# Random-feature attention with a mixture of experts on one core: copies of normalized rows issued by GpSimd, and two counts in one PSUM bank

## The chip, the cores and the metric

The kernel runs on one core of one Trainium2 chip. A core has TensorE (PE, matrix products into PSUM), VectorE (DVE), ScalarE (ACT), GpSimd (POOL) and SyncE (SP, which here only issues DMAs), all with queues of their own. ScalarE and GpSimd can issue DMAs too. The metric is the device time of one execution in microseconds, lower is better.

## The reference

The input is 8192 tokens of 512 numbers. Cut to what matters:

```python
xn = layernorm(x)
feats = rfs(xn)                       # 512 features: exp of a projection less a norm
attn  = feats @ weights.T             # weights: the same features of 512 input rows
# the mixture of experts
scores = sigmoid(xn @ router_w)       # 64 experts in 8 groups
#   the best 4 groups, in them the best 8 experts per token; their weights sum to 2.5
#   each expert takes its first 256 tokens, in order of tokens
dispatch[e, pos] = xn[token]
expert_out = (silu(dispatch @ gate_w) * (dispatch @ up_w)) @ down_w
moe = sum of weight * expert_out, and a shared expert on all tokens
out = x + attn + moe
```

The position of a token in an expert is a running count over all earlier tokens. Everything is float32.

## The kernel before

**Precision.** A matmul operand is split into a high part (rounded to float32r by a ScalarE copy, `upper`, line 98) and a residual (VectorE, `rest`, line 101). `products` (line 108) adds three products: high by high, high by low, low by high.

**Stages.** Tokens go in 16 blocks of 512. In the first stage, up to some 405 us, the routing of every block is computed (`look_up`, lines 343 to 484) and, for the even blocks, the shared expert and the attention (`dense`, lines 513 to 565). The second stage, up to some 1161 us, runs the 64 experts: GpSimd gathers an expert's rows by indirect DMA (`gather`), TensorE transposes and multiplies them, and GpSimd adds the results to the output by indirect DMA. The attention of odd blocks (`late_attention`) is spread over it. The third finishes the odd blocks.

**The order of work.** `look_up` and `dense` are generators that one loop advances by hand: `routing` (line 841) is called once per step of `dense`, advances every open `look_up` by one step, begins a new one every five steps, and two steps before that calls `normalize` for it. So a pair of blocks, an odd one and the next even one, passes during the ten steps of one even block's `dense`. What is written this way sets priorities. The tile library then fixes the order of instructions on each engine when the program is built, gives out the buffers of a pool in the order of the program, and sets the semaphores. On the chip each engine keeps to its order, and a DMA that waits holds up what is behind it on the engine that issues it.

**A block's path.** `statistics` (VectorE) and `roots` (line 281: 17 small operations on GpSimd) give a token's scale and shift. ScalarE writes the normalized rows into `xw` (line 301); a row has 577 numbers, since the router's results and a sum come behind the 512. From block 5 on (`ROUND`), each of a block's two `xw` tiles (two times 128 rows) is copied within SBUF into a tile `xc` of 512 columns by a DMA that ScalarE issues (line 314). The copy is of type float32 and is read as float32r by the transposes (line 331, tile `ps_x`), 16 a block. From there on the block is `xT`, high and low parts, two of whose four PSUM buffers come from the pool `ps_sm`.

One step later the router's matmul fills `ps_l` (line 364), copied to `lt` by ScalarE (line 374), transposed back into `ps_lt` (line 381), and VectorE finds groups and experts (lines 397 to 438): `mask_r` says who takes which expert, `prior_r` counts takers in the partition's rows before. Two steps later TensorE makes two sums of these: `ps_b` (line 443), each expert's count before each group of 128 tokens, and `ps_u` (line 454), the count up to each token, transposed. ScalarE copies `ps_u` to `cu` (line 462) and SP stores it. In the next step VectorE adds comparisons of `ps_b` to `begun` (line 482, two operations), from which the second stage finds each expert's tokens.

**PSUM.** The pools have 2, 4 and 2 banks. `ps_sm`, with two, holds in turn two `ps_x`, `ps_b`, `ps_u`, the next block's `ps_l` and its `ps_lt`: six tiles a block, all with the tag "sm".

Of the kernel before, what the change touches and what calls it, by code (L numbers as in the profile page):

```python
# [9 lines left out]
FP = mybir.dt.float32  # L10
# [8 lines left out]
P = 128  # L19
T = 8192  # L20
H = 512
R = 512
E = 64
# [8 lines left out]
TB = 512  # L32
NB = T // TB
NS = TB // P
# [19 lines left out]
def rfs_attention_moe_kernel(  # L54
# [15 lines left out]
    nc = tc.nc  # L70
# [6 lines left out]
    ps_sm = ctx.enter_context(tc.tile_pool(name="ps_sm", bufs=2, space=PSUM))  # L77
# [6 lines left out]
    def kib4(shape, name, dt=FPR):  # L84
        return four.tile(shape, dt, tag="four", name=name)
# [31 lines left out]
    def behind(a, b):  # L117

        tc.add_manual_dep(a.ins, b.ins.name, ORDER, reason="what a needs comes late")
# [38 lines left out]
    def store_rows(b, k, xb):  # L158

        r0 = b * TB + k * UT  # L160
        return nc.sync.dma_start(
            out[r0 : r0 + UT, :].rearrange("(s p) d -> p s d", p=P), xb.t[k]
        )
# [133 lines left out]
    def normalize(b, rstd, shift):  # L297
        xb = xbs[b]
        xw = [rows.tile([P, NH, XW], FP, tag="xw", name="xw") for _ in range(NS // NH)]
        for s in range(NS):  # L300
            normed_s = nc.scalar.activation(
                xw[s // NH][:, s % NH, :H],
                xb[s],
                AF.Identity,
                bias=shift[:, s : s + 1],
                scale=rstd[:, s : s + 1],
            )
            behind(normed_s, last["upper"])
        xc = None
        if b >= ROUND:  # L310

            xc = [kib4([P, NH, H], "xc", FP) for _ in xw]
            for t, w in zip(xc, xw):
                nc.scalar.dma_start(t, w[:, :, :H])
        if b % 2:

            for k in range(TB // UT):
                store_rows(b, k, xb)
            del xbs[b]
        return xw, xc  # L320
# [22 lines left out]
    def look_up(b):  # L343
# [90 lines left out]
        for s in range(1, NS):  # L434
# [4 lines left out]
        yield  # L439
        yield  # L440

        pb = ps_sm.tile([P, NS, E], FP, tag="sm", name="ps_b")
        counted = nc.tensor.matmul(
            pb.rearrange("p s e -> p (s e)"),
            ones_r,
            prior_r.rearrange("p s e -> p (s e)"),
            start=True,
            stop=True,
        )
        behind(counted, last["pe"])  # L450
        pu = ps_sm.tile([P, NS // 2, P], FP, tag="sm", name="ps_u")
        for q in range(NS // 2):
            for part, (w, v) in enumerate(((mask_r, tri_r), (prior_r, ones_r))):
                nc.tensor.matmul(
# [172 lines left out]
    rest(rwp[:, :, 1, :], rw_sb, rwp[:, :, 0, :], nc.gpsimd)  # L627
    normed = {}
    normed[0] = normalize(0, *roots(0, statistics(xbs[0], NS * [last["rest"]]), nc.vector))
    first = last["shift"]  # L630
    roots1 = roots(1, statistics(xbs[1], NS * [first]))
# [20 lines left out]
    for rc in range(RC):  # L652
        pool, tag = ((ps_sm, "sm"), (ps_tr, "tr"))[rc // 2]
        ps_w.append(pool.tile([P, H], FP, tag=tag, name="ps_f"))
        projected(parts(wT, KC), rc, ps_w[rc])
    late = look_up(0)
    next(late)
    upper0 = last["upper"]
    sup = split(sgu[1], "gu", (upper0, last["rest"]))
    fw = Chunks(RC, "fw", FP)  # L660
    for rc in range(RC):
        exponents = exponent(fw[rc], wn, rc, ps_w[rc])
        behind(exponents, last["rest"])
    normed[1] = normalize(1, *roots1)
    eab = const.tile([P, RC], FP, name="eab")
    behind(nc.scalar.activation(eab, ab, AF.Exp), upper0)
# [174 lines left out]
    def routing(t):  # L841

        for b in sorted(fronts):
            if next(fronts[b], fronts) is fronts:
                del fronts[b]
        b, k = divmod(t + GAP, GAP)
        if k == (b == 1) and b < NB:
            fronts[b] = look_up(b)
            next(fronts[b])
        if k == GAP - 3 and b + 1 < NB:  # L850
            normed[b + 1] = normalize(b + 1, *roots(b + 1, statistics(xbs[b + 1])))
        if k == 1 and b + 2 < NB:
            xbs[b + 2] = load_tokens(b + 2)
# [141 lines left out]
```

## Time and profile before

| | us |
|---|---|
| median of 3 runs | 1320.38 |
| lowest and highest | 1320.17, 1323.96 |
| the profiled execution | 1324.84 |
| its span | 1323.1 |
| first stage, 33 to 405 us: PE busy | 363.93 of 372 |
| second stage, 405 to 1161 us: PE busy | 752.71 of 756 |
| third stage, 1161 to 1323 us: PE busy | 156.65 of 162 |
| first stage: DVE, ACT, POOL busy | 286.66, 165.07, 52.91 |

In the rows of a profile, a tile stands without its number. "out<-in xN" names what an instruction writes and reads and how many are taken together; a timeline row begins with its start and its length in us, and ends in brackets with the idle time before it and what ended that. "ACTq" and "SPq" are DMAs as issued by ScalarE and SP, "PEld" a weight load of TensorE. [...] A row of waits has the total in us, how many times, and the longest. TensorE's matmuls overlap, so that the length of a row is more than the time it takes from the next. TensorE's clock was granted at 0.998 of full speed.

### The profile page before, as it was taken

How to read it: one execution, taken by the hardware profiler on the slowest of the kernel's cores; microseconds unless marked ns; L12 is line 12 of the kernel's file. 1: busy time of each engine (PE TensorE's matmuls, PEld its weight loads, DVE VectorE, ACT ScalarE, POOL GpSimd, SP SyncE). 2: the span in 40 equal slices, each digit the busy share in tenths (PEclk: the TensorE clock that was granted, in tenths of full speed). 3: DMA queues.
4: the chain of work that ended last, by engine and by line, in shares of the span. 5: the costliest groups of instructions: out<-in, count | busy, mean ns of one | idle time of the engine just before them, and what ended most of it. 6: DMA issues, size and time to landing. Idle time of an engine off the chain costs nothing.

```text
span 1323.1 us, 21351 instructions
## 1 busy us (share of the span) xinstructions
PE 1300.0 (98%) x7648; PEld 1138.6 (86%) x7648; DVE 929.2 (70%) x1922; ACT 646.1 (49%) x1017; POOL 573.1 (43%) x670
## 2 busy tenths in 40 slices
PE   8999999999999999999999999999999999999998
PEld 6888787788788899999999999999999999988886
DVE  7978768768765677777677767777776776643555
ACT  5644443444332455656556556655565565540111
POOL 3122012012105667778667676767677754210000
PEclk9999999999999999999999999999999999999999
DMA  7665675675585989999999999999999999875995
GB/s 253 239 229 198 234 259 197 233 266 209 193 314 178 305 216 306 270 276 271 317 271 264 309 265 283 248 294 285 266 259 303 281 259 234 227 220 178 317 319 191
DMA packets 192313, 338.60 MB, mean 256 GB/s; under 512 B 15952, under 2 KB 87632, under 8 KB 192208
## 3 DMA queue, kind: packets, MB, share of 16 engines
q1 hardware_dynamic: 153456, 245.93, 54.1%
q0 software_dynamic: 32768, 79.78, 27.3%
q10 hardware_dynamic: 5984, 11.54, 2.5%
q8 instruction: 60, 0.98, 0.3%
q14 instruction: 45, 0.37, 0.1%
HBM read 220.66 MB, written 104.99 MB: 246 GB/s over the span
## 4 chain that ended last, share of the span: by engine, by line
PE 90%; DVE 4%; DMA 4%; ACT 1%; issue 1%; POOL 0%; SPq 0%; DVEq 0%; ACTq 0%
PE ps_gu L108 41%; PE ps_o L108 14%; PE ps_e L108 13%; PE ps_fu L108 6%; PE ps_y L108 5%; PE ps_f L108 3%; PE ps_t L769 3%; DMA xc<-xw 2%; PE ps_l L364 2%; PE ps_x L331 2%; DMA xb<-in_L_attn_x_dram 1%; DVE f L491 0%; DVE r L499 0%; DVE fT L101 0%; DVE st L275 0%
## 5 line engine op out<-in xcount | busy, mean ns | idle before, releaser
L819 POOL DMA_INDIRECT out_dram<-ye,who x128 | 225.5, 1762 | 186.5 <-ACT ye L818 136.4
L108 PE MATMUL ps_gu<-gT,gu_h 128*128 128x256 f32 x2048 | 291.3, 284 | 0.0
L108 PEld LDWEIGHTS ps_gu<-gT,gu_h 128*128 128x128 f32 x2048 | 268.6, 192 | 5.3 <-ACT gu_h L98 1.0
L699 POOL DMA_INDIRECT at<-upto,line x128 | 140.2, 1095 | 80.1 <-DMA q<-norms 41.4
L108 PE MATMUL ps_gu<-gT,gu_l 128*128 128x256 f32 x1024 | 167.3, 286 | 0.2 <-DVE gu_l L101 0.2
L101 DVE TENSOR_TENSOR gu_l<-gu,gu_h 128x1024 fp32r<-128x1024 f32 x128 | 155.6, 1218 | 6.9 <-ACT gu_h L98 6.9
L752 POOL DMA_INDIRECT xg<-xnw,who x128 | 143.1, 1118 | 39.0 <-issue 32.6
L108 PE MATMUL ps_e<-d_h,ehT 128*128 128x512 f32 x512 | 148.6, 392 | 0.0
L108 PEld LDWEIGHTS ps_gu<-gT,gu_l 128*128 128x128 f32 x1024 | 140.9, 192 | 0.7 <-DVE gu_l L101 0.4
L98 ACT CAST gu_h<-gu 128x1024 fp32r<-128x1024 f32 x128 | 132.5, 1058 | 0.0
L246 POOL TENSOR_TENSOR a<-rstd,ve 128x4 f32<-128x4 f32 x45 | 10.5, 233 | 272.0 <-DVE rstd L242 269.6
L98 ACT CAST ehT<-sg 128x512 fp32r<-128x512 f32 x64 | 39.8, 621 | 156.6 <-DVE sg L499 153.7
L818 ACT ACTIVATE ye<-ps_e,we 128x512 f32<-128x512 f32 x128 | 88.6, 695 | 56.4 <-PE ps_e L108 55.6
L108 PEld LDWEIGHTS ps_e<-d_h,ehT 128*128 128x128 f32 x512 | 94.7, 188 | 18.8
L499 DVE SCALAR_TENSOR_TENSOR sg<-sg,ps_gu 128x512 f32<-128x512 f32 x64 | 44.0, 688 | 68.4 <-PE ps_gu L108 68.2
L101 DVE TENSOR_TENSOR d_l<-d,d_h 128x1024 fp32r<-128x1024 f32 x64 | 78.3, 1224 | 7.6 <-ACT d_h L98 7.2
L101 DVE TENSOR_TENSOR gT<-ps_t,gT 128x512 fp32r<-128x512 f32 x128 | 83.2, 682 | 0.0
L101 DVE TENSOR_TENSOR ehT<-sg,ehT 128x512 fp32r<-128x512 f32 x64 | 44.4, 694 | 51.8 <-ACT ehT L98 51.8
L505 ACT ACTIVATE f<-f,ab 128x512 f32<-128x512 f32 x64 | 46.4, 725 | 69.3 <-DVE f L491 69.3
L108 PE MATMUL ps_o<-fW_h,fT 128*128 128x512 f32 x288 | 79.3, 392 | 0.2 <-ACT fT L98 0.2
L108 PE MATMUL ps_e<-d_l,ehT 128*128 128x512 f32 x256 | 79.4, 391 | 0.0
L108 PE MATMUL ps_o<-d_h,hT 128*128 128x512 f32 x256 | 78.3, 396 | 0.0
(180 smaller groups left out, 2513.6 us busy)
## 6 DMA issues: line engine op xcount, KB each, us to landing
gu<-in_L_ffn_gate_w_dram SPq DMA_DIRECT2D x64, 512.0 KB
gu<-in_L_ffn_up_w_dram SPq DMA_DIRECT2D x64, 512.0 KB
d<-in_L_ffn_down_w_dram SPq DMA_DIRECT2D x64, 512.0 KB
xnw<-xw SPq DMA_DIRECT2D x32, 577.0 KB
xb<-in_L_attn_x_dram SPq DMA_DIRECT2D x32, 512.0 KB
out_dram<-xb SPq DMA_DIRECT2D x32, 512.0 KB
xT_h<-turned SPq DMA_DIRECT2D x30, 512.0 KB
xT_l<-turned SPq DMA_DIRECT2D x30, 512.0 KB
```

The costliest lines, as they stand in the source:

```text
L98: return nc.scalar.copy(dst, src)
L101: return on.tensor_tensor(dst, src, hi.bitcast(FP), ALU.subtract)
L108: last["pe"] = nc.tensor.matmul(ps, w[c][a], v[c][b], start=(start and part == 0 and c == 0), stop=(stop and part == 2 and c == n - 1),)
L331: last["turn"] = nc.tensor.transpose(pr[:, ts(s, P)], src(s)[:, ts(kc, P)], ident if dt is FP else ident_r)
L364: logits = nc.tensor.matmul(pl, rwp[:, kc].rearrange("p t e -> p (t e)"), v[kc], start=(n == 0 and kc == 0), stop=(n == 1 and kc == KC - 1),)
L499: nc.vector.scalar_tensor_tensor(dst, dst, 0.5, u, ALU.mult, ALU.mult)
L505: nc.scalar.activation(f, f, AF.Exp, scale=ab[:, rc : rc + 1])
L699: nc.gpsimd.indirect_dma_start(out=at[:, e % TE, h, :], out_offset=None, in_=upto, in_offset=bass.IndirectOffsetOnAxis(ap=line[:, e, h : h ...
L752: nc.gpsimd.indirect_dma_start(out=xgs[e][:, h, :], out_offset=None, in_=xnw, in_offset=bass.IndirectOffsetOnAxis(ap=who[:, e, h : h + 1], ...
L769: turned_s = nc.tensor.transpose(pr[:, c, ts(h, P)], xr[:, h, ts(c2 * 2 + c, P)], ident_r)
L818: nc.scalar.activation(ye[:, h, :], po, AF.Copy, scale=wes[e][:, h : h + 1])
L819: now = nc.gpsimd.indirect_dma_start(out=out, out_offset=bass.IndirectOffsetOnAxis(ap=who[:, e, h : h + 1], axis=0), in_=ye[:, h, :], in_o ...
```

## The change

Two edits. In `normalize` the two copies of a block are issued from GpSimd's queue and no more from ScalarE's. In `look_up` one tile of one PSUM bank, 512 numbers wide, is taken from `ps_sm` in place of two tiles; its first half is `pb`, its second `pu`. The matmuls and their readers are the same.

```diff
             xc = [kib4([P, NH, H], "xc", FP) for _ in xw]
             for t, w in zip(xc, xw):
-                nc.scalar.dma_start(t, w[:, :, :H])
+                nc.gpsimd.dma_start(t, w[:, :, :H])
...
-        pb = ps_sm.tile([P, NS, E], FP, tag="sm", name="ps_b")
+        both = ps_sm.tile([P, 2, TB // 2], FP, tag="sm", name="ps_bu")
+        pb = both[:, 0].rearrange("p (s e) -> p s e", e=E)
         counted = nc.tensor.matmul(
-            pb.rearrange("p s e -> p (s e)"),
+            both[:, 0],
             ones_r,
             prior_r.rearrange("p s e -> p (s e)"),
             start=True,
             stop=True,
         )
         behind(counted, last["pe"])
-        pu = ps_sm.tile([P, NS // 2, P], FP, tag="sm", name="ps_u")
+        pu = both[:, 1].rearrange("p (q t) -> p q t", t=P)
```

## The prediction

> **What bounds the kernel now.** I read the page's busy shares first, then TensorE's waits, then the timelines around the two places that the change touches.
>
> ```profile
> PE 1300.0 (98%) x7648; PEld 1138.6 (86%) x7648; DVE 929.2 (70%) x1922; ACT 646.1 (49%) x1017; POOL 573.1 (43%) x670
> ...
> PE 90%; DVE 4%; DMA 4%; ACT 1%; issue 1%; POOL 0%; SPq 0%; DVEq 0%; ACTq 0%
> ```
>
> TensorE (PE) is the bound: busy 98% of 1323.1 us and 90% of the chain that ended last. So an edit is worth what it takes out of PE's idle time, some 23 us in all, and work taken off ScalarE (49%) is worth nothing by itself. All that the diff touches runs in the first third, where PE waits little; these are its waits from 33 to 405 us (PE's matmuls, and PEld, its weight loads):
>
> ```profile
> PEld ps_x L331 <- DMA xc<-xw: 5.7, 5, 1.6
> PEld ps_l L364 <- ACT cu L462: 4.5, 7, 0.6
> PEld ps_l L364 <- issue: 3.2, 5, 0.6
> ```
>
> Columns: total us, times, longest. The first row is the copy of normalized rows that lands after PE wants to transpose it. The next two stand ahead of the router's matmul (ps_l, L364), once a block. Both places are the diff's.
>
> **Part 1: the copies (L314).** There are 22, two in each of the blocks 5 to 15. They behave in two ways. In even blocks (6, 8, 10, 12, 14; here block 6):
>
> ```profile
> 134.81 1.54 ACT L301 ACTIVATE xw<-xb,shift,rstd 128x512 f32<-128x512 f32 x2
> ...
> 143.86 0.66 ACTq L314 DMA_DIRECT2D xc<-xw  x1
> ...
> 145.58 0.65 ACTq L314 DMA_DIRECT2D xc<-xw  x1
> ```
>
> The rows are ready at 136.35 (134.81 + 1.54), yet ScalarE issues the copies 7.5 and 9.2 us later, because they stand in its queue behind copies that wait for PE and VectorE (lt at 140.49, f at 143.10, L388 at 144.38). PE meets the second copy too early:
>
> ```profile
> 150.75 0.28 PE L331 MATMUL ps_x<-ident_r,xc 128*128 128x128 f32 x2
> 151.92 0.28 PE L331 MATMUL ps_x<-ident_r,xc 128*128 128x128 f32 x1 [0.89 <-DMA xc<-xw]
> ```
>
> By the matmuls' start records the five losses are 1.03, 1.64, 0.83, 0.92 and 1.32, sum 5.7 us, the PEld row's total. GpSimd has nothing to do then: its timeline ends at 125.27 with the roots of block 6 and goes on at 164.28. So it can issue at about 136.4. Block 6's transposes come at 150.75, 14 us later; no transfer in the numbers below takes so long. I take **-5.7 us** for the even blocks. What could still hold them there is the SBUF slot that a copy writes, if its last user is late; ScalarE's queue hides whether that is so now.
>
> In odd blocks (5 to 15; here block 7) it is the other way round:
>
> ```profile
> 172.04 0.60 ACTq L314 DMA_DIRECT2D xc<-xw  x1
> ...
> 178.39 1.47 PE L331 MATMUL ps_x<-ident_r,xc 128*128 128x128 f32 x16
> ```
>
> ScalarE issues as soon as the rows are there, PE needs them 6.35 us later and waits for nothing. But GpSimd is busy just then: it computes the roots of block 8 from 169.18 to 173.64 (17 operations of some 0.28 us). On that queue the second copy starts at 172.04 at the earliest and, if both go behind the roots, at 173.64 plus the first copy's issue, 175.6. What a plain copy from GpSimd costs, no row shows; the nearest are the gathers, which GpSimd issues too:
>
> ```profile
> 414.26 1.01 POOL L699 DMA_INDIRECT at<-upto,line  x1 [0.30 <-issue]
> ...
> 428.44 0.95 POOL L752 DMA_INDIRECT xg<-xnw,who  x1 [0.31 <-issue]
> ...
> 435.69 1.96 POOL L752 DMA_INDIRECT xg<-xnw,who  x1 [0.30 <-issue]
> ```
>
> Issuing takes 0.95 to 1.96 us. The first of these is the last of eight that VectorE waits for at 417.77: 3.5 us from issue to use, with the queues fairly empty. The second is used by PE at 435.06: 6.6 us, under load. An xc copy is 512 KB in 256 rows, more than either, so I allow 1 us more at the light end: 4.5 to 6.6 us. Landing is thus 176.5 at best (no loss) and 182.2 at worst (3.8 us lost). SP's stores start at 174.44, behind the copies if these are issued early. I take issue at 174.0 and 4.9 us, that is 178.9, **0.5 us lost in each of six odd blocks, +3.0 us**; the ends are 0 and about 23.
>
> [...] The rows: 0.95 us alone, 1.96 us at 435.69 while VectorE ran the residual of the weights (L101, two SBUF inputs) from 434.48 to 436.83, a factor of two. [...]
>
> Behind the copies on GpSimd stand the roots of the next block. Block 8's last shift is done at 173.17 and ScalarE uses it at 181.75: 8.6 us of slack against at most 3.9 us of issuing. Cost nothing; without that slack 3.9 us in five blocks. SP's queue keeps its own order, nothing is moved past it. ScalarE loses 22 issues of 0.60 us, 13.2 us, of an engine with idle time: nothing.
>
> **Part 2: one PSUM bank for ps_b and ps_u.** The pool has two banks. Now the two counts take both, and the next block's ps_l has to wait until one is read:
>
> ```profile
> 160.21 0.28 PE L454 MATMUL ps_u<-ones_r,prior_r 128*128 128x128 f32 x1
> 160.32 0.68 PE L108 MATMUL ps_o<-fW_l,fT 128*128 128x512 f32 x2
> 161.25 0.94 PE L364 MATMUL ps_l<-xT_h,rwp 128*128 128x512 f32 x3 [0.24 <-DVE xw L471]
> ```
>
> A 512-column matmul enters every 0.227 us (four from 158.68 to 159.59). Two from 160.32 would let the next in at 160.77; it enters at 161.25, just after begun (L482, done 161.10) or cu (L462, done 160.90) frees a bank. The idle figures count this twice over (PEld 0.6, PE 0.2); the start records give 0.38 to 0.41 us in 12 blocks and 0.25 in one, 5.0 us in all. With one bank for both counts, ps_l takes the other, whose last reader is the VectorE residual of the transposes, done at 158.0. So **-5.0 us**; the ends are 0 (if the low half of the transposes comes late instead) and 5.0.
>
> It adds a wait. [...] Now begun (160.13 to 161.10, VectorE) and cu (160.53 to 160.90, ScalarE) overlap, in different banks. [...] Behind it on VectorE stand statistics and the next f (L491), for which VectorE sat idle 3.49 us at 142.32; PE's accumulators wait for f. [...] The next taker of the shared bank is ps_lt, which needs the lt copy (163.37 to 163.96) anyway, later than begun. Cost nothing.
>
> **Sum.** The profiled execution took 1324.84 us, 1.7 around its span, and is 4.5 us (0.3%) over the median, 1320.38. 1324.84 - 5.7 - 5.0 + 3.0 = 1317.1; the same 7.7 us off the median give **1312.7 us**.
>
> **Rivals.** A change under 0.3% (4.0 us) can't be told from none, so faster is under 1316.4 and slower over 1324.3.
>
> (a) Both stalls go and odd copies cost 0 to 1 us each: 1309.7 to 1315.7, likeliest 1312.7. For it: the idle GpSimd in even blocks and the free bank. Against: one unmeasured latency. Chance 0.60.
>
> (b) The stall moves: odd copies cost 1.1 to 2.4 us each, 6.6 to 14.4, which eats the gain. For it: GpSimd's queue holds the next roots just then, and SP's 1.6 MB of stores at 174.44. Time about 1319. Chance 0.15.
>
> (c) The second part doesn't do what it says, as ps_l in PE's queue then waits for something else (xT_l, or VectorE held up by begun): 1320.4 - 5.7 + 3.0 = 1317.7. Against: xT_l is done 2 us before. Chance 0.10.
>
> (d) Slower: odd copies land late under load. It decides from 14.7 us in six blocks, 2.45 us each, that is a landing at 180.8 in block 7. With both issued behind the roots (175.6) and the loaded 6.6 us it is 182.2, 3.8 us in each: 1320.4 - 10.7 + 22.8 = 1332.5; a mean of this case is 1329. Against: PE's order is fixed when the program is built, and a transpose that is planned later lets other matmuls go ahead. Chance 0.15.
>
> **How the numbers follow.** Faster: nearly all of (a), a little of (b) and (c), 0.63. Same: most of (b) and (c), 0.21. Slower: (d) and the edge of (b), 0.16. The range, 1308.5 to 1324.3, leaves out (d) and a rest below, under 2 in 10; (a)'s own is 1309.7 to 1315.7.
>
> **What the new profile would show.** Right: no wait of ps_x for xc in even blocks, and copies issued within 1 us after the rows; no wait of ps_l for cu, and ps_l straight after ps_u; begun after cu. Wrong: a row of ps_x waiting for xc in odd blocks, five or six times over 1 us; copies on GpSimd taking over 2 us each; ScalarE's xw waiting longer for the shift; PE waiting for f.

## The result and the profile after

The changed kernel takes 1311.7 us (median of six runs, 1310.29 to 1317.16) against 1320.28 us for the kernel before in the same session (1319.47 to 1323.96): 0.9936 of the time, 95% interval 0.9919 to 0.9952. In a later session the ratio was 0.9923 (0.9902 to 0.9944). The forecast was 1312.7. The profiled execution took 1313.35 us, with a span of 1311.6.

The busy shares and the chain, then TensorE's waits from 33 to 405 us, of the kernel after (lines behind the first edit have moved by 2 or 3: `ps_b` and `ps_u` are now `ps_bu`, lines 445 and 456):

```profile
PE 1296.5 (99%) x7648; PEld 1138.3 (87%) x7648; DVE 925.1 (71%) x1922; ACT 645.5 (49%) x1017; POOL 582.4 (44%) x692
...
PE 89%; DVE 6%; DMA 2%; SPq 1%; issue 1%; ACT 1%; POOL 0%; ACTq 0%; DVEq 0%
```

```profile
PEld ps_bu L445 <- issue: 3.1, 6, 0.7
...
PE ps_bu L445 <- DVE prior_r L435: 1.0, 4, 0.3
PE ps_lt L381 <- ACT lt L374: 0.9, 2, 0.7
```

Both old rows are gone: no row shows `ps_x` waiting for a copy or `ps_l` for a bank. New ones have come: in six places TensorE reaches the counts (`ps_bu`) a little before VectorE has finished `prior_r`.

Block 6, an even one, on ScalarE, GpSimd and TensorE (three timelines of the kernel after):

```profile
133.18 1.55 ACT L301 ACTIVATE xw<-xb,shift,rstd 128x512 f32<-128x512 f32 x2
...
135.03 0.77 POOL L314 DMA_DIRECT2D xc<-xw  x1 [5.55 <-ACT xw L301]
136.93 0.72 POOL L314 DMA_DIRECT2D xc<-xw  x1 [1.12 <-ACT xw L301]
...
150.62 1.49 PE L331 MATMUL ps_x<-ident_r,xc 128*128 128x128 f32 x16
```

The first tile is ready at 134.73 and its copy is issued at 135.03. The sixteen transposes come in one piece, 14 us after the second copy's issue. Block 7, an odd one:

```profile
168.87 0.78 POOL L314 DMA_DIRECT2D xc<-xw  x1 [1.38 <-ACT xw L391]
169.67 0.21 POOL L246 TENSOR_TENSOR a<-rstd,ve 128x4 f32<-128x4 f32 x1
...
170.75 0.77 POOL L314 DMA_DIRECT2D xc<-xw  x1 [0.31 <-ACT top L467]
171.55 0.24 POOL L249 TENSOR_TENSOR rstd<-a,rstd 128x4 f32<-128x4 f32 x1
...
176.83 1.49 PE L331 MATMUL ps_x<-ident_r,xc 128*128 128x128 f32 x16
```

The copies stand before and among the roots of block 8, not behind them. GpSimd is idle for 1.38 us ahead of the first, until ScalarE's rows are there, and the root behind it goes only then. Both land 3.2 us after issue, the second at 173.95, and TensorE needs them at 176.83. Block 5 has no such room: its second copy, issued at 124.30, lands at 130.02, and the transpose that reads it starts at 130.06, 0.1 us late. Over all 22 copies, the view of the tile `xc` says:

```profile
L314 POOL DMA_DIRECT2D xc<-xw x22: 724/770/982, 122.9 to 358.7; - x22
...
DMA to landing us min/median/max: 3.2/4.6/7.2
```

The three numbers of the first row are the shortest, median and longest duration in ns: a plain copy holds GpSimd for 0.72 to 0.98 us. The counts and what follows, on TensorE, then on ScalarE and VectorE:

```profile
157.98 0.36 PE L445 MATMUL ps_bu<-prior_r,ones_r 128*128 128x256 f32 x1
...
158.46 0.27 PE L456 MATMUL ps_bu<-ones_r,prior_r 128*128 128x128 f32 x1
158.57 1.15 PE L364 MATMUL ps_l<-xT_h,rwp 128*128 128x512 f32 x4
```

```profile
158.77 0.37 ACT L464 COPY cu<-ps_bu 128x256 f32<-128x256 f32 x1 [3.67 <-PE ps_bu L456]
...
159.63 0.47 DVE L484 SCALAR_TENSOR_TENSOR begun<-ps_bu,slot,begun 128x256 f32<-128x256 f32 x1
```

`ps_l` enters straight after the last sum of the second count. `begun` now stands behind `cu`, and VectorE isn't idle ahead of it: other work filled the time.

**Where the time went.** For each profile I added up TensorE's losses from the matmuls' start records: the excess of each distance between two starts over the median distance of the same pair of kinds. In us:

| profile | first stage (33 to 405) | start of the second (405 to 470) | rest |
|---|---|---|---|
| before, the first profile | 13.5 | 5.5 | 9.5 |
| before, again | 11.6 | 1.4 | 9.1 |
| after, the first profile | 4.5 | 2.8 | 9.1 |
| after, again | 3.5 | 2.0 | 9.1 |

The first stage loses 9.0 us less in the first pair and 8.1 in the second. The level of such a sum depends on how the kinds are drawn; a second measure, the time that TensorE takes for the same number of matmul columns, gives 9.0 and 7.9. The rest of the first pair's 11.5 us of span is the start of the second stage, where neither copy nor count is at work; in the second pair, after is 0.6 us worse there.

### The profile page after: what moved, and what is told of

Its sections match the earlier page's. It is cut to its first block, busy times and chain, and to the rows that moved or that the text cites. A ratio compares the mean times of both kernels' runs of the same rounds, so it can differ in the third digit from the quotient of the medians.

```text
span 1311.6 us, 21365 instructions
## 1 busy us (share of the span) xinstructions
PE 1296.5 (99%) x7648; PEld 1138.3 (87%) x7648; DVE 925.1 (71%) x1922; ACT 645.5 (49%) x1017; POOL 582.4 (44%) x692
## 4 chain that ended last, share of the span: by engine, by line
PE 89%; DVE 6%; DMA 2%; SPq 1%; issue 1%; ACT 1%; POOL 0%; ACTq 0%; DVEq 0%
PE ps_gu L108 41%; PE ps_e L108 13%; PE ps_o L108 12%; PE ps_fu L108 6%; PE ps_y L108 5%; PE ps_f L108 3%; PE ps_t L771 3%; PE ps_x L331 2%; PE ps_l L364 1%; DMA xb<-in_L_attn_x_dram 1%; DVE st L275 1%; SPq L262 1%; DVE f L493 1%; DVE xT_l L101 1%; DMA q<-norms 1%
## 5 line engine op out<-in xcount | busy, mean ns | idle before, releaser
L754 POOL DMA_INDIRECT xg<-xnw,who x128 | 138.6, 1083 | 39.0 <-issue 31.7
```

What stands on the lines that cost most here:

```text
L754: nc.gpsimd.indirect_dma_start(out=xgs[e][:, h, :], out_offset=None, in_=xnw, in_offset=bass.IndirectOffsetOnAxis(ap=who[:, e, h : h + 1], ...
```

## The experiments

The runs come from three sessions, each on one chip with the kernel before beside it. In the first and third, the kernel before itself took 1334 and 1336 us, not 1320; so ratios hold within a session, and the first stage's losses are the closer measure across them.

**The copies alone**, twice. The second run was made because the first had a long stall elsewhere.

```diff
# the kernel before
-                nc.scalar.dma_start(t, w[:, :, :H])
+                nc.gpsimd.dma_start(t, w[:, :, :H])
```

> The copies alone go to GpSimd; the two counts keep their two banks. Theory (two separate sets of TensorE stalls): the five waits of ps_x for xc in even blocks, 5.7 us, go, and nothing comes in odd blocks, so 1314.6 us, a ratio of 0.9957; ps_l still loses 0.4 us a block. Rival (the gain of both parts is really the bank's, and a stall at ps_x would only be caught up later): no change, 1320.

> The copies alone on GpSimd, once more, since the first run of this edit had a stall of 15 us where the second stage begins, at a place that no copy and no count touches. My theory: that stall belongs to the chip of that call (its run of the kernel before was 13 us longer too), and on another chip the edit is worth what it showed in the first stage, 5.5 to 7.5 us, and no odd block pays: 0.9945 to 0.996 of the time before. Rival: the planner's other order, made by the copies, makes the stall on any chip: 0.998 to 1.001. The prediction's steps: -5.7 and +3.0, 0.998.

Measured: 0.9995 (0.9977 to 1.0012), then 0.9949 (0.9936 to 0.9962). In both the first stage loses 6.1 us, and `ps_x` waits for no copy, in even or odd blocks. What is left there is the bank, in half the blocks (waits of the first run):

```profile
PEld ps_l L364 <- ACT cu L462: 4.7, 8, 0.6
```

By start records it costs 2.9 us, not the 5.0 of before. With the copies early, the library orders TensorE otherwise in odd blocks: the counts go some matmuls earlier, and their banks are read in time. So this edit alone is worth 7.4 us against the first profile of before (13.5 - 6.1): 5.4 of copies and 2.1 of bank. My first expectation, a ratio of 0.9957, was missed in the first run, which hid the gain behind 22.8 us lost from 405 to 470 us, 15.2 of them in one wait.

**The shared bank alone**, twice.

```diff
# the kernel after
-                nc.gpsimd.dma_start(t, w[:, :, :H])
+                nc.scalar.dma_start(t, w[:, :, :H])
```

> The shared bank alone; ScalarE issues the copies. Theory: the losses ahead of ps_l, 5.0 us, go, and the new waits of ps_bu for prior_r, 1.7 us in the changed kernel's records, come, so 1317.0 us, a ratio of 0.9975, and the waits of ps_x for xc stay near 5.7 us. Rival (the bank is worth all the 8.6 us): 1312. Rival (new waits eat it all): 1320.

> The shared bank alone, copies from ScalarE as before, once more. My theory: 3 to 4 us in the first stage (the five waits of ps_x for xc stay, no wait of ps_l for a bank, a new wait of ps_bu for prior_r in a few blocks): 0.997 to 0.998 of the time before. The prediction's step: -5.0 us, 0.9962. Rival: begun behind cu costs something on VectorE, and this is 1.0 or more.

Measured: 0.9973 (0.996 to 0.9985), then 0.9959 (0.9946 to 0.9972); the first stage loses 9.6 and 7.9 us. The waits of the second run:

```profile
PEld ps_x L331 <- DMA xc<-xw: 5.8, 5, 1.5
```

The copies' stall is whole. The bank's is gone: ahead of `ps_l` start records show 0.3 us in all, against 5.0, and the counts wait for `prior_r` only once. Against the first profile of before this edit alone is worth 3.9 us (with 1.6 us of slow clock after one stall in that run, of which below) and 5.6. With the 7.4 of the copies that would be 11.3 to 13.0, and together they are worth 9.0: the first part takes 2.1 us of the second's gain and puts the counts of odd blocks where `prior_r` can be late, up to 1.7 us.

**Copies from GpSimd in even blocks only**, first on the kernel before, then on the changed one.

```diff
# the kernel before; in the changed one the first line has nc.gpsimd
-                nc.scalar.dma_start(t, w[:, :, :H])
+                (nc.scalar if b % 2 else nc.gpsimd).dma_start(t, w[:, :, :H])
```

> Two banks as before; GpSimd issues the copies of even blocks, ScalarE those of odd blocks. Theory (the place in ScalarE's queue is the cause, and only even blocks stand badly there): the same as with all copies on GpSimd, 1314.6 us. Rival (the gain is ScalarE's freed issue time, 0.6 us a copy, all blocks alike): half of the gain, 1317.5.

> The changed kernel, but odd blocks' copies are issued from ScalarE as before; the order on TensorE is that of the changed kernel. It takes the predicted +3.0 us of the odd blocks away, if that was real. My theory: the odd copies cost nothing on GpSimd, so this takes the same time as the changed kernel within 0.15% (2 us), 0.993 to 0.996 of the time before, and ps_x waits for no xc in either. The prediction's step: 3.0 us less than the changed kernel, 0.991 to 0.992. Rival: ScalarE's queue is the better place for nothing, and this is slower by what ScalarE's work behind the issues loses, 1 to 3 us.

Measured: 0.9951 (0.9938 to 0.9964) with two banks for the counts, and 0.992 (0.9898 to 0.9941) with one. The first stage loses 6.1 and 3.6 us, the same as with all copies on GpSimd (6.1 and 3.5). On one chip the changed kernel took 1311.39 us and this one 1310.90, and the runs of the two overlap. The predicted 3.0 us of the odd blocks are not there.

**The first count in another pool's bank**, with the copies on GpSimd: does it take a shared bank, or only a free one?

```diff
# the copies alone
-        pb = ps_sm.tile([P, NS, E], FP, tag="sm", name="ps_b")
+        pb = ps_tr.tile([P, NS, E], FP, tag="tr", name="ps_b")
```

> All copies on GpSimd, and ps_b in a bank of the transposes' pool in place of a bank shared with ps_u, so that begun need not come behind cu. Theory (what matters is that the counts leave one of the two banks of ps_sm to ps_l): no wait of ps_l for cu, a time near that of the change, 1312 us. Rival (the order begun behind cu costs VectorE something that reaches TensorE): 1 to 3 us better than the change. Rival (a bank of the transposes' pool is missed there): over 1315.

Measured: 0.9961 (0.9949 to 0.9972), 6.2 us lost in the first stage, no better than the copies alone. So my theory was missed, and the second rival held. The wait for `cu` is gone, and another stands in its place:

```profile
PEld ps_l L364 <- DVE xT_l L101: 3.5, 7, 0.6
```

The count now takes a buffer from the transposes. A bank freed by taking one elsewhere moved the stall; sharing one removed it.

**Each copy twice**, the first time into a spare tile.

```diff
# the kernel after
-                nc.gpsimd.dma_start(t, w[:, :, :H])
+                nc.gpsimd.dma_start(kib4([P, NH, H], "xs", FP), w[:, :, :H])
+                nc.gpsimd.dma_start(t, w[:, :, :H])
```

> The changed kernel with each copy issued twice from GpSimd, first into a spare tile that nobody reads, so that GpSimd's issues (0.77 us each) and the bytes moved by these copies double. My theory: the odd blocks have slack on GpSimd's queue and in the transfer; the second real copy is issued some 1.5 us later and lands 1.5 to 3 us later; 0 to 1 us is lost in each of the six odd blocks, nothing in even ones: 0 to 6 us over the changed kernel, 0.994 to 0.998 of the time before. Rival (the slower case of the prediction): the odd copies are at the edge, and doubled they are 2.5 us or more late in each block with the roots behind them late too: 15 us or more over the changed kernel, 1.005 or more.

Measured: 1336.39 us, 1.0102 (1.0078 to 1.0127), 25 us over the changed kernel. My expectation of at most 6 us was wrong. The first stage loses 24.0 us, and `ps_x` waits for its copies in five of the six odd blocks. Block 7 again, on GpSimd, then on TensorE:

```profile
175.28 0.78 POOL L314 DMA_DIRECT2D xs<-xw  x1 [1.61 <-ACT xw L301]
176.05 0.74 POOL L314 DMA_DIRECT2D xc<-xw  x1
176.77 0.74 POOL L314 DMA_DIRECT2D xs<-xw  x1
177.49 0.74 POOL L314 DMA_DIRECT2D xc<-xw  x1
```

```profile
183.21 0.28 PE L331 MATMUL ps_x<-ident_r,xc 128*128 128x128 f32 x2
185.12 1.40 PE L331 MATMUL ps_x<-ident_r,xc 128*128 128x128 f32 x14 [1.63 <-DMA xc<-xw]
186.36 1.89 PE L108 MATMUL ps_gu<-xT_h,gu_h 128*128 128x512 f32 x4
188.04 1.91 PE L108 MATMUL ps_gu<-xT_l,gu_h 128*128 128x512 f32 x4
```

The issues cost little: measured back from the transposes, the second real copy is issued 5.7 us ahead, against 6.1 in the changed kernel's run on the same chip. But it takes 7.6 us to land, where it took 3.2. Twice the bytes are under way, and SP's stores (from 177.72) come in among them; which of the two costs more isn't shown. The last two rows show a second loss, in the distance of their starts: four matmuls of 512 columns take 1.68 us where they took 0.91. By stretches of time (the length of the stretch, busy time of PE, PEld, DVE, ACT and POOL, then the granted clock, the DMA share and GB/s):

```profile
183.00:186.30 3.30, 1.67 (x18) 1.44 (x16) 1.53 (x3) 1.39 (x3) 0.00 (x0) 1.00 1.02 382
186.30:189.70 3.40, 3.40 (x11) 2.68 (x10) 2.45 (x5) 2.69 (x5) 0.42 (x1) 0.53 0.75 291
```

After the stall the clock is granted at 0.53 over these 3.4 us, which loses as much again (start records: 1.77 us of stall, 1.67 of slow clock). Over the five blocks the stalls are 10.2 us and the slow clock, in four of them, 6.3: 16.5 of the 20.5 us that this kernel lost beyond the changed one in the first stage. The other 4.0 us are small waits that I did not follow.

**The counts one step later**, to spare the new wait for `prior_r`.

```diff
# the kernel after, look_up
         nc.vector.tensor_tensor(taken, prior[:, NS - 1, :], mask[:, NS - 1, :], ALU.add)
         yield
         yield
+        yield
```

> The changed kernel with the two counts one step later in a block's routing, so that prior_r is long done when TensorE comes to them. My theory: the waits of ps_bu for prior_r were what the shared bank cost, 1 to 2 us, and go: 0.9915 to 0.9925 of the time before, 0 to 1.5 us less than the changed kernel, and the new plan's losses elsewhere stay under 1 us. Rival: the counts then meet other work in the two banks of the pool, with a wait of ps_l or ps_lt of 0.4 us or more a block, and it is slower than the changed kernel by 3 us or more (0.995).

Measured: 1.0046 (1.0033 to 1.0059). The waits for `prior_r` are gone, yet the first stage loses 17.6 us, by neither of the ways expected. The order of the program is new, and in it GpSimd gets the copies of block 7 behind all the roots of block 8 (GpSimd, then TensorE):

```profile
175.71 0.22 POOL L294 TENSOR_SCALAR padded<-q 128x4 f32<-128x4 f32 x1
176.28 1.50 POOL L314 DMA_DIRECT2D xc<-xw  x2 [0.34 <-issue]
```

```profile
184.60 1.39 PE L331 MATMUL ps_x<-ident_r,xc 128*128 128x128 f32 x14 [2.47 <-DMA xc<-xw]
```

The rows were ready at 173.65 (ScalarE's last `xw` starts at 171.43 and takes, as a row of three, 2.22 us), so the copies are 2.6 us late. The second, issued at 177.1, lets TensorE go on at 184.60, 7.5 us later. TensorE stands for 2.47 us, with the clock granted at 0.70 over the 3.6 us from there. This is the prediction's slower rival, in place and mechanism. The row for the whole first stage:

```profile
PE ps_x L331 <- DMA xc<-xw: 8.9, 6, 2.5
```

These waits, and some 5 us of slow clock behind three of them, are nearly all of the 14.1 us that this kernel loses beyond the changed one in the first stage.

**The copies from SP's queue.** TensorE, VectorE and ScalarE keep the changed kernel's orders.

```diff
# the kernel after
-                nc.gpsimd.dma_start(t, w[:, :, :H])
+                nc.sync.dma_start(t, w[:, :, :H])
```

> The changed kernel with the copies issued from SP's queue; the orders of TensorE, VectorE and ScalarE are those of the changed kernel, and GpSimd has only its roots in the first stage. SP's queue holds the loads of x, and stores that wait for their tiles. My theory: what matters is that nothing ahead of the copies waits; on SP the stores of the turned block before stand ahead in some blocks, so that one or both copies of a block are issued 1 to 5 us later than on GpSimd, and ps_x waits in some blocks: 0.993 to 0.998 of the time before. Rival: any queue but ScalarE's will do, and this takes the changed kernel's time within 0.15%.

Measured: 0.9934 (0.992 to 0.9948), the changed kernel's gain, and `ps_x` waits for nothing. The first stage loses 2.3 us, the least of all. The row of the copies:

```profile
L314 SPq DMA_DIRECT2D xc<-xw x22: 594/602/697, 123.0 to 356.6; - x22
```

I expected copies held up behind SP's stores, and in even blocks they are: SP issues them 4.8 to 6.8 us after the rows are ready (in block 6 at 141.71; the store of `cu`, issued at 138.86, and others stand ahead). But that is still 7.0 us or more ahead of the transposes, so nothing is lost; in ScalarE's queue block 6's copies were 7.5 and 9.2 us late. So GpSimd isn't what helps; leaving ScalarE's queue is, and a queue with some delay does too. The order of TensorE is that of the changed kernel, yet the counts lose nothing to `prior_r` here, which is most of the difference from its 3.5 to 4.5 us; why they don't isn't shown. SP's queue also holds no roots that a new order could put ahead.

**The kernel before, and the changed kernel, once more**, with no edit.

> The kernel before, unchanged, profiled on this chip so that its stages can be set beside those of the variants. My theory: TensorE loses 13.5 us against its median pace in the first stage, as in the first profile (within 1 us), and the stall where the second stage begins (410 to 445 us) is a matter of the run or of the chip and not of the edits, so it shows some 5 to 10 us here too, against 2.9 in the first profile. Rival: the variants' different plans make that stall, and the kernel before shows 3 us there on any chip.

> The changed kernel, unchanged, on the same chip as the next two. My theory: 0.9936 of the time before (0.992 to 0.996); the first stage loses 4.5 us, 9 less than before; ps_x waits for no xc; ps_bu waits some 0.3 to 0.5 us in a few blocks for prior_r. Rival: the gain of the first stage is eaten where the second begins, as in the run with the copies alone, and the ratio is 0.998 to 1.0.

Measured: 1319.55 us (one execution) for the kernel before; 1311.39 and 0.9923 (0.9902 to 0.9944) for the changed one. The kernel before loses 11.6 us in the first stage, not 13.5 within 1 us as expected, because its copies came less late:

```profile
PEld ps_x L331 <- DMA xc<-xw: 3.6, 5, 0.9
```

The theory that the start of the second stage would lose 5 to 10 us on this chip too fell: it lost 1.4 us, and 2.0 in the changed kernel. The rival, that the plans of the variants make that stall, fell too: the runs with even copies only (one bank) and with doubled copies ran here with other plans and lost 0.8 and 4.3 us. On the two chips with a slower kernel before, all eight variants lost 16.0 to 22.8 us there; the kernel before was not profiled on those. In the run with SP's queue it looks like this (VectorE, then TensorE):

```profile
410.76 1.21 DVE L718 TENSOR_REDUCE tok<-at 128x8 f32<-128x1024 f32 x1
417.93 0.75 DVE L493 SCALAR_TENSOR_TENSOR f<-q,ab,ps_fu 128x512 f32<-128x512 f32 x1 [5.96 <-remote]
```

```profile
420.14 0.79 PE L108 MATMUL ps_y<-fW_h,fU 128*128 128x512 f32 x1 [6.02 <-ACT fU L98]
```

VectorE stands for 5.96 us although the matmuls that its next instruction reads had all entered by 409.2. "Remote" means that the profile knows of no instruction or queue that ended the wait. So the stall goes with the chip, or with the session, and not with the edits. What makes it stays open.

## Why the prediction was right

The forecast was 1.0 us over the median, and its mechanism held in the first stage, where the profiles show 9.0 and 8.1 us against the predicted 7.7. But two terms were off, one by 3.0 us too dear and one by about 1.5 too large a gain, and their errors partly cancelled. That much of the closeness is luck.

- **Even blocks, -5.7 us: right in kind, and in size for the profile it was read from.** Taken against its median distance, `ps_x` lost 5.4 us between its matmuls in the first profile of before (5.7 as the prediction counted) and nothing after. The second profile of before, counted in the first way, shows 3.3: how late a copy lands differs between two executions of one kernel, so the term was one draw. In the two runs of the shared bank alone it was again 5.4 to 5.6.
- **Odd blocks, +3.0 us: measured 0.** No odd block waits over 0.1 us, and issuing their copies from ScalarE gives no more. Three inputs were too dear. The issue costs 0.77 us at the median, where I took 0.95 to 1.96 from the gathers; the landing in block 7 was 3.2 us, where I took 4.9; and the copies got ahead of most roots, the second issued at 170.75, where I took 174.0. Block 5, where the landing takes 5.7 us, is at the edge.
- **The shared bank, -5.0 us: right alone, too large beside the first part.** With the bank alone the loss ahead of `ps_l` fell from 5.0 to 0.3 us. In the changed kernel the first part had taken 2.1 of it already, through TensorE's order in odd blocks, and the counts then lost up to 1.7 us to `prior_r`. The step that failed was to cost each edit in the order of before and add.
- **`begun` behind `cu`, cost nothing: right.** In block 6's row `begun` starts 0.49 us after `cu` ends, with VectorE busy until then. In all of the first stage VectorE waited for `cu` once, 0.2 us. It hangs on the order: with the counts one step later it waits for `cu` seven times, 6.7 us, up to 1.0 each, and no loss of TensorE was traced to that.
- **Roots behind the copies, cost nothing: right, though the sign that I named against it appears.** ScalarE's `xw` waits for the shift five times, 15.1 us in all (from 125 us on), against 1.8 before. But the copies on GpSimd aren't its cause: with them on SP's queue it is 15.1 us too, and with the shared bank alone, where ScalarE issues them, 13.8. Before, ScalarE had stood there for `pen` instead, 13.4 us, and no wait of TensorE was found behind it.
- **GpSimd's issue beside VectorE's work, weighed by the row of 1.96 us: cheaper than that row.** All 22 issues lie between 0.72 and 0.98 us, with VectorE busy 284 of the first stage's 372 us. Why the gather of that row took twice the 0.95 us of an earlier one isn't shown.
- **The slower rival was real, with its deciding point set too high.** In the changed kernel its place has 2.9 us of room in block 7, and none in block 5. With doubled copies, or with another order, the first stage loses 20.5 and 14.1 us more than the changed kernel's 3.5, and the time grows by 25.0 us, and by 15.8 (the latter against the copies from SP's queue, in the same session). And it would have decided earlier than at the 2.45 us a block that I gave: behind a wait of 1.63 us the clock doubled the loss (1.77 us of stall, 1.67 of slow clock).

## What to carry to other kernels

In these runs a DMA was issued only after what stood ahead of it in its engine's queue (7.5 and 9.2 us after the rows in ScalarE's in block 6, 4.8 to 6.8 us in SP's in even blocks): before moving one, list what stands ahead in the new queue in the order of the program, and when the data is needed, since copies placed behind the next block's roots (2.6 us late in block 7) turned the gain into a loss (1.0046). Two edits that free the same engine in the same stage need not be a sum, because the order is planned anew for each. Where a variant is measured at one end of the kernel, compare the losses stage by stage, so that a stall of the chip elsewhere isn't taken for the edit's.

## What the runs showed of the hardware

- **Short stalls of TensorE were followed by half clock in some places and not in others.** Waits of 1.63 us (doubled copies) and 2.47 us (counts later) were followed by half clock for 3.41 us in the clock records. A wait of 1.50 us in the kernel before, and one of 1.44 with doubled copies, were not (granted at 1.00 from 200.5 to 208 us, and from 337 to 340.5); one of 1.41 with the shared bank alone was (0.71 over the 3.5 us after it). So it isn't the length alone. Within a trace the slow stretches start on one grid with steps of 3.413 us. Adding up TensorE's idle time in each step of that grid (stalls of over 0.3 us by start records, which put a stall some 0.1 us above the wait in a row's brackets), in the ten runs that have a slow stretch before their end, separates the cases: in the first stage no step with up to 1.36 us was followed by a slow one, and all eight with 1.49 us or more were. (At the start of the second stage 19 of 21 were.) The 1.50 us wait was spread over two steps, with 0.96 us at most in one; of the 1.44 us wait 1.36 fell into one. In the first stage of the changed kernel no single stall is over 0.51 us.
- **The time of a copy within SBUF differed with what else was under way:** in block 7 3.2 us to landing, with the DMA engines busy 83% of that time, and 7.6 among doubled copies and SP's stores, with them busy all of the time from 179.0 us on (a share of 1.02), at the same size and from the same engine.
- **The same kernel's time differed by 1% between sessions on different chips:** 1320 and 1321 us in two of them, 1334 and 1336 in the others. Most of it seems to lie in 65 us at the start of the second stage, where eight profiles of variants from the slower chips lose 16.0 to 22.8 us and six profiles from the other sessions 0.8 to 5.5.
